# A planned four-layer graph kernel: bank preference in the planner, one opening of four block products, eps inside the squares, a later preamble step

## The chip, the core and the metric

The kernel runs on one core of one Trainium2 chip. A core has a matrix engine (TensorE, PE in the profile, with its weight loads shown apart as PEld), a vector engine (DVE), an activation engine (ACT), a general engine (POOL) and a queue for transfers (SP). Each engine works through its own instructions in a fixed order; semaphores make one engine wait for another. Matmul results land in PSUM, which is used here as eight banks of 128 x 512 fp32 values. The metric is the device time of one execution in microseconds, the median of several runs.

## The reference

The input is x, 64 graphs of 256 nodes with 128 features, and one 256 x 256 adjacency matrix A for all of them; everything is fp32. Four layers follow each other, and after each comes a layer norm of "x plus the layer":

```
layer 0: x W0 + sum over k=1..3 of (A^k x)(Wk + Wk+3)      x = LN(x + layer0)
layer 1: A (x W) + b                                        x = LN(x + layer1)
layer 2: D^-1/2 (A + I) D^-1/2 x W^T + b                    x = LN(x + layer2)
layer 3: h = x; five times:
           m = A h;  u = h U3^T + b
           z = sigmoid([m, m] W3^T + b + u);  r = sigmoid([m, m] W4^T + b + u)
           hv = tanh([m, m] W5^T + b + (r h) U5^T + b)
           h = (1 - z) h + z hv                             x = LN(x + h)
LN(v) = (v - mean) / sqrt(var + 1e-5) over the features
```

## The kernel before

**Tiling.** The 64 graphs are cut into 32 groups of two; a group is named by the number of its first graph (0, 2, 4 to 62). A group's activations fill one tile of 128 x 512: two graphs, two halves of the nodes, 128 features. Ten groups are in work at a time (`ACTIVE`), so that PE always finds a group that is ready. For later groups, transposed copies are made by a DVE transpose, a store to device memory and a load back (`tx`, `dx`, `xT` for the input; `th`, `dh`, `h` or `hT` in the steps of layer 3; `tn`, `dn`, `hn` at the end).

**The product with A.** `propagate` multiplies a tile by A. With both operands cut into 2 x 2 blocks, `seven` does this with seven block products in place of eight. POOL makes the sums of blocks of h (`ts01`, `ts2`, `ts3`, tiles `ts` and `tq`); the sums of A's blocks (`s_aT`, `s_a2T`, `s_anT`, `s_aTp`) are made once, on DVE, in the preamble (`block_sums`). The products share one bank, `ps` (in the profile `pmq`, `pm`, `pmg` for layer 0, layers 1 and 2, and layer 3). PE does them in four calls: `first` is one product and opens the bank, `middle` is the three that use POOL's sums, `more` is one that is added onto the first, `rest` is two. Between them ACT copies the first product (`us`), because `more` then changes it, DVE forms the sums `post11`, `post12`, `post13` and `post2` (L642, L645, L648, L652), and ACT copies a part of the bank into `m` (L664). `rest` writes where DVE and ACT read before, so it waits for them.

**Gates.** In a step of layer 3, `pr` gets two products, with m (`w4`) and with hT (`u3`); ACT makes r; DVE makes rh = r hT; `ph` gets products with m and with rh (the `u5` product); `pr` gets one more with m (`w34`), which turns it into the input of z. Then ACT makes z and hv, and DVE makes d = hv - hT, e = z d and the new hT (all L729).

**Norms.** The weights are centred in the preamble so that the outputs of the layers have mean zero. `normalise_centred` then needs only the mean square: four `Square` activations on ACT with scale C^-1/2 and an accumulated sum (L515; C is 128), EPS added on POOL (L519), the power -1/2 on POOL (L520), four scalings on ACT (L531). The last six groups end in `closing`, which gathers h and y by matmuls into a bank `s` and takes the same way, with the final product on DVE (L574). The other groups of the last layer use bn_stats on DVE (`statistics`, L491 to L502, L551).

**What sets the order.** Nothing is written out by hand: each piece of work is an `Op` with an engine, a cost in ns, a lag, a rank, a function that issues it, and the tiles that it reads and writes. `Plan.order` simulates the engines. It takes again and again, over all engines, the operation with the smallest key, and so fixes the order on each engine as well as the slot that each tile gets:

```
key = (max(at, t0), op.rank, op.seq)
```

`at` is when the inputs are ready and a slot of each needed kind is free, `t0` when the engine is free, and the rank of a group's operation is its number (for the last seven groups nearly equal, with a part that grows as the group moves on). Of the operations that could start at the same time the oldest group's goes first. Preamble operations (`pre`) have ranks of their own: -9 and -8 for A transposed and squared (aT, a2T), -7 for the first layer's weights (`w0s`), 0.3 for the normalised adjacency (`degree`, the power, `rows` L334, the PE transpose `p_an` L259, `columns` L338), 2.1 for the transposed weights of later layers (`transposed`, tiles `p_w2u3T` and `p_w435u5T`). The transposes into `p_w2u3T` use two loads, raw_w2 and raw_u3.

Of the kernel before, what the change touches and what calls it, by code (L numbers as in the profile page):

```python
# [8 lines left out]
F32 = mybir.dt.float32  # L9
AF = mybir.ActivationFunctionType  # L10
OP = mybir.AluOpType
AX = mybir.AxisListType

P = 128
# [9 lines left out]
EPS = 1e-5  # L24
# [26 lines left out]
class Plan:  # L51
# [32 lines left out]
    def order(self):  # L84
        free = {}
        pool = {k: [(0.0, i) for i in range(n)] for k, n in self.slots.items()}
        left = {op: len(op.deps) for op in self.ops}
        placed = {op: [v for v in op.vals if v.kind != "const"] for op in self.ops}
        after = {op: [] for op in self.ops}
        for op in self.ops:  # L90
            for d in op.deps:
                after[d].append(op)
        open_ = {}
        ready = {}
        for op in self.ops:
            if not left[op]:
                ready.setdefault(op.engine, []).append((0.0, op))
        done = []
        while any(ready.values()):
            best = None  # L100
            for e, waiting in ready.items():
                t0 = free.get(e, 0.0)
                pick = None
                for at, op in waiting:
                    need = {}
                    for v in placed[op]:
                        if v.slot is None:
                            need[v.kind] = need.get(v.kind, 0) + 1
                    short = False
                    for k, n in need.items():  # L110
                        if len(pool[k]) < n:
                            short = True
                            break
                        at = max(at, sorted(pool[k])[n - 1][0])
                    if short:
                        continue
                    key = (max(at, t0), op.rank, op.seq)
                    if pick is None or key < pick[0]:
                        pick = (key, op)
                if pick and (best is None or pick[0] < best[0]):  # L120
                    best = pick
            assert best, "the plan is stuck"
            (start, _, _), op = best
            ready[op.engine] = [w for w in ready[op.engine] if w[1] is not op]
            op.start, op.end = start, start + op.cost + op.lag
            free[op.engine] = start + op.cost
            for v in placed[op]:
                if v.slot is None:
                    pool[v.kind].sort()
                    v.slot = pool[v.kind].pop(0)[1]  # L130
                    open_[v] = len(v.users)
                open_[v] -= 1
                if not open_[v]:
                    pool[v.kind].append((max(u.end for u in v.users), v.slot))
            for n in after[op]:
                left[n] -= 1
                if not left[n]:
                    at = max(d.end for d in n.deps)
                    ready.setdefault(n.engine, []).append((at, n))
            done.append(op)  # L140
        assert len(done) == len(self.ops)
        return sorted(done, key=lambda op: (op.start, op.seq))


def pe_cost(columns, n=1):
    return n * 2 * (max(columns, P) / 1.2 + 2)
# [11 lines left out]
def kernel(  # L158
# [30 lines left out]
    nc = tc.nc  # L189
    B, N, C = x.shape  # L190
# [43 lines left out]
    half = const.tile([P, Q], F32, name="half")  # L234
    nc.vector.memset(half, -0.5)


    early = constant("early", [P, Q])
    pre(-9, "ACT", 1500, lambda: nc.scalar.activation(early.ap, half, AF.Sigmoid), [], [early])
# [44 lines left out]
    w0s = constant("w0s", [P, 4, C])  # L284
# [55 lines left out]

    pre(0.3, "DVE", 1500, degree, [a_nat], [ahat, deg])
    pre(0.3, "POOL", 700, lambda: nc.gpsimd.tensor_tensor(dinv.ap, deg.ap, half[:, :T], op=OP.pow), [deg], [dinv])
    pre(0.3, "DVE", 600, rows, [ahat, dinv], [ahat])
    pre(0.3, "PE", 4 * 110, lambda: turn(p_an, ahat), [ahat], [p_an])
    pre(0.3, "DVE", 900, columns, [p_an, dinv], [anT])


# [92 lines left out]
    class Group:  # L440
# [68 lines left out]
        def spread_of(self, tag, s):  # L509

            y, ve, rs = self.val("w", "y" + tag), self.val("ve", "ve" + tag), self.val("rs", "rs" + tag)

            def squares():
                for q in range(self.q):
                    nc.scalar.activation(nat(y)[:, q, :], nat(s)[:, q, :], AF.Square, scale=C ** -0.5,  # L515
                                         accum_out=ve.ap[:, q:q + 1])

            def scales():
                nc.gpsimd.tensor_scalar(ve.ap, ve.ap, EPS, None, op0=OP.add)  # L519
                nc.gpsimd.tensor_tensor(rs.ap, ve.ap, half[:, :self.q], op=OP.pow)  # L520

            self.act(squares, [s], [y, ve], 295 * self.q)
            self.add("POOL", 1330, 100, scales, [ve], [ve, rs])
            return y, rs

        def normalise_centred(self, tag, s):
# [66 lines left out]
        def seven(self, tag, h, aTs, ins, blocks):  # L593

            sums = sums_of[aTs]
            ps, m = self.val("bank", "pm" + tag), self.val("w", "m" + tag)
            ts, tq, u = self.val("th", "ts" + tag), self.val("q", "tq" + tag), self.val("th", "us" + tag)
            w = self.val("q", "ws" + tag)  # L600

            def row(v, k):
                return v.ap[:, k * P:(k + 1) * P]

            def o(v, q, blocks=blocks):
                if v.kind == "q":
                    return v.ap.rearrange("p (k i) -> p k i", k=4)
                if blocks:
                    return v.ap.rearrange("p (k q i) -> p q k i", k=4, i=32)[:, q]
                return v.ap.rearrange("p (q k i) -> p q k i", k=4, i=32)[:, q]  # L610


            def ts01():
                nc.gpsimd.tensor_tensor(ts.ap[:, :2 * P].rearrange("p (x c) -> p x c", x=2), ins(h)[:, 1], ins(h)[:, :, 0],  # L614
                                        op=OP.subtract)

            def ts2():
                nc.gpsimd.tensor_tensor(row(ts, 2), ins(h)[:, 1, 1], row(ts, 0), op=OP.subtract)

            def ts3():  # L620
                nc.gpsimd.tensor_tensor(tq.ap, row(ts, 2), ins(h)[:, 0, 1], op=OP.subtract)

            def block(q, w, a, start=False):
                mm(row(ps, q), w, a, start, True, shared=True)

            def first():
                block(0, ins(h)[:, 0, 0], aTs.ap[:, 0, :P], True)

            def middle():
                block(2, row(ts, 0), sums.ap[:, 0, :])  # L630
                block(1, row(ts, 1), sums.ap[:, 2, :])
                block(3, row(ts, 2), sums.ap[:, 1, :])

            def more():
                block(0, ins(h)[:, 0, 1], aTs.ap[:, 1, :P])

            def rest():
                block(2, ins(h)[:, 1, 1], sums.ap[:, 3, :])
                block(1, tq.ap, sums.ap[:, 4, :])

            def post11():
                nc.vector.tensor_tensor(row(u, 0), row(u, 1), row(ps, 3), op=OP.add)  # L642

            def post12():
                nc.vector.tensor_tensor(row(w, 0), row(u, 0), row(ps, 1), op=OP.add)  # L645

            def post13():
                nc.vector.tensor_tensor(o(m, 3), o(w, 0, False), o(ps, 2, False), op=OP.add)  # L648

            def post2():  # L650
                both = o(u, 0, False)[:, None].to_broadcast([P, 2, 4, 32])
                nc.vector.tensor_tensor(o(m, slice(1, 3)), o(ps, slice(1, 3), False), both, op=OP.add)  # L652

            started = self.pe(pe_cost(P, 1), first, [h, aTs], [ps])
            kept = self.act(lambda: nc.scalar.copy(row(u, 1), row(ps, 0)), [ps], [u], 165)
            self.add("POOL", 830, 100, ts01, [h], [ts])
            self.add("POOL", 610, 100, ts2, [h, ts], [ts])
            self.add("POOL", 590, 100, ts3, [h, ts], [tq])
            self.pe(pe_cost(P, 3), middle, [ts, sums], [ps], True, (started,))
            self.pe(pe_cost(P, 1), more, [h, aTs], [ps], True, (kept,))  # L660
            self.dve(post11, [ps, u], [u], 215)
            self.dve(post12, [ps, u], [w], 215)
            self.dve(post13, [ps, w], [m], 215)
            self.act(lambda: nc.scalar.copy(o(m, 0), o(ps, 0, False)), [ps], [m], 165, True)  # L664
            self.pe(pe_cost(P, 2), rest, [h, tq, sums], [ps], True)
            self.dve(post2, [ps, u], [m], 340, True)
            return m
# [245 lines left out]
```

## Time and profile before

Time before: 1354.72 us, the median of three runs (1353.41 to 1354.8). The profiled execution spans 1350.3 us from the first to the last instruction.

| engine | busy us | share of the span | instructions |
|---|---|---|---|
| PE (matmul) | 1336.5 | 99% | 6553 |
| PEld (weights) | 928.3 | 69% | 6553 |
| DVE | 940.9 | 70% | 2304 |
| ACT | 758.1 | 56% | 2421 |
| POOL | 680.7 | 50% | 1097 |

Matmuls overlap in the engine's pipeline, so a PE that is busy 99% of the time isn't by that at its peak: the distance from one matmul's start to the next tells more than its duration. A line of the timeline gives start and duration in us, engine and line of the kernel, the output tile, the inputs, the shapes and the count; in brackets stands how long the engine was idle before, and what ended it. A line of the groups gives the total busy time and the mean of one in ns, and after the next bar the idle time before. Transfers are 134.96 MB in all, and the queue engines are busy a third of the time.

### The profile page before, as it was taken

The page shows a single profiled execution, that of the slowest core. Times are in us where ns is not written, and L with a number is a line of the kernel's source. Part 1 is how long each engine was busy: PE and PEld are TensorE (multiplying, and loading weights), DVE is VectorE, ACT ScalarE, POOL GpSimd, SP SyncE. Part 2 cuts the span into 40 slices and gives each one's busy share as a digit, 9 for nine tenths or more (in the row PEclk, how much of TensorE's full clock was granted, in tenths as well). Part 3 has the DMA queues.
Part 4 walks back from the last instruction along what each step waited for, and adds up shares of the span by engine and source line. Part 5 has one row for each costly group of instructions (what it writes and reads, how often), then busy time and mean ns, then how long its engine had stood idle before and what let it go on. Part 6 is the DMA issues. An engine that isn't in the chain of part 4 may idle for free.

```text
span 1350.3 us, 22012 instructions
## 1 busy us (share of the span) xinstructions
PE 1336.5 (99%) x6553; PEld 928.3 (69%) x6553; DVE 940.9 (70%) x2304; ACT 758.1 (56%) x2421; POOL 680.7 (50%) x1097
## 2 busy tenths in 40 slices
PE   8999999999999999999999999999999999999997
PEld 7886666676776766677666666676776776565554
DVE  5466677767667667865676776676666677877776
ACT  4675536467654556556565554474655686444445
POOL 5785425266742566247266443383653686233323
PEclk9999999999999999999999999999999999999999
DMA  6322334242522333333233433341332223333323
GB/s 175 109 71 71 94 94 128 77 128 78 147 78 77 111 95 118 115 106 100 64 110 110 127 100 98 94 137 56 110 102 63 82 85 121 87 106 95 93 78 110
DMA packets 269495, 134.96 MB, mean 100 GB/s; under 512 B 175776, under 2 KB 241056, under 8 KB 269376
## 3 DMA queue, kind: packets, MB, share of 16 engines
q1 hardware_dynamic: 269120, 133.42, 34.1%
q8 instruction: 53, 0.87, 0.3%
q14 instruction: 66, 0.54, 0.1%
q0 software_dynamic: 256, 0.13, 0.1%
HBM read 67.31 MB, written 65.80 MB: 99 GB/s over the span
## 4 chain that ended last, share of the span: by engine, by line
PE 95%; DVE 1%; DMA 1%; ACT 1%; issue 0%; SPq 0%; POOLq 0%; ACTq 0%; POOL 0%; DVEq 0%
PE pr L199 31%; PE ph L199 20%; PE pmg L199 19%; PE py L199 15%; PE pm L199 7%; PE pmq L199 3%; DMA x<-in_x_dram 1%; DMA w_raw<-in_L_gnn_weight_dram 0%; PE s L199 0%; DMA dx<-tx 0%; ACT y L515 0%; ACT y L551 0%; DVE s L543 0%; SPq L748 0%; DVE tx L745 0%
## 5 line engine op out<-in xcount | busy, mean ns | idle before, releaser
L199 PE MATMUL pr<-mg,w435u5T 128*128 128x512 f32 x640 | 319.8, 593 | 0.0
L614 POOL TENSOR_TENSOR tsg<-h 128x256 f32<-128x256 f32 x128 | 97.2, 760 | 292.5 <-DMA h<-dh 197.5
L722 ACT ACTIVATE r<-pr,bsum 128x512 f32<-128x512 f32 x160 | 109.7, 685 | 151.5 <-PE pr L199 150.7
L722 ACT ACTIVATE pr<-pr,bsum 128x512 f32<-128x512 f32 x160 | 105.5, 660 | 112.4 <-PE pr L199 109.3
L729 DVE TENSOR_TENSOR rh<-r,hT 128x512 f32<-128x512 f32 x160 | 122.7, 767 | 61.6 <-ACT r L722 60.7
L199 PE MATMUL ph<-rh,w435u5T 128*128 128x512 f32 x320 | 163.6, 594 | 0.0
L199 PE MATMUL ph<-mg,w435u5T 128*128 128x512 f32 x320 | 163.3, 592 | 0.0
L199 PE MATMUL pr<-hT,w2u3T 128*128 128x512 f32 x320 | 163.0, 593 | 0.0
L729 DVE TENSOR_TENSOR d<-ph,hT 128x512 f32<-128x512 f32 x160 | 109.7, 686 | 76.1 <-ACT ph L722 73.0
L199 PEld LDWEIGHTS pr<-mg,w435u5T 128*128 128x128 f32 x640 | 109.4, 191 | 65.3 <-issue 53.3
L722 ACT ACTIVATE ph<-ph,bsum 128x512 f32<-128x512 f32 x160 | 105.6, 660 | 60.4 <-PE ph L199 59.9
L531 ACT ACTIVATE y<-s,rs 128x128 f32<-128x128 f32 x384 | 122.1, 392 | 11.0 <-POOL rs L520 10.7
L515 ACT ACTIVATE y<-s 128x128 f32<-128x128 f32 x396 | 116.7, 299 | 16.9 <-DVE s L538 14.9
L199 PEld LDWEIGHTS pmg<-s_aTp,tsg 128*128 128x128 f32 x768 | 101.8, 192 | 33.5 <-issue 28.5
L652 DVE TENSOR_TENSOR mg<-pmg,usg 128x256 f32<-128x256 f32 x160 | 67.0, 419 | 72.7 <-PE pmg L199 70.4
L199 PEld LDWEIGHTS pmg<-aTp,h 128*128 128x128 f32 x512 | 87.1, 197 | 39.4 <-issue 29.2
L729 DVE TENSOR_TENSOR pr<-pr,d 128x512 f32<-128x512 f32 x157 | 108.7, 692 | 1.5
L520 POOL TENSOR_TENSOR rs<-ve,half 128x4 f32<-128x4 f32 x99 | 104.1, 1052 | 8.3
L519 POOL TENSOR_SCALAR ve<-ve 128x4 f32<-128x4 f32 x99 | 23.2, 234 | 166.6 <-ACT y L515 166.3
L729 DVE TENSOR_TENSOR hT<-hT,pr 128x512 f32<-128x512 f32 x157 | 106.1, 676 | 1.3
L199 PE MATMUL pmg<-s_aTp,tsg 128*128 128x128 f32 x768 | 106.2, 275 | 0.0
L642 DVE TENSOR_TENSOR usg<-usg,pmg 128x128 f32<-128x128 f32 x160 | 45.2, 284 | 81.7 <-PE pmg L199 47.7
(181 smaller groups left out, 2816.9 us busy)
## 6 DMA issues: line engine op xcount, KB each, us to landing
dh<-th SPq DMA_DIRECT2D x160, 256.0 KB, 2.0
h<-dh SPq DMA_DIRECT2D x256, 128.0 KB, 2.5
x<-in_x_dram SPq DMA_DIRECT2D x32, 256.0 KB, 3.4
hT<-dh SPq DMA_DIRECT2D x128, 64.0 KB, 2.0
out_dram<-y SPq DMA_DIRECT2D x32, 256.0 KB, 2.3
dx<-tx SPq DMA_DIRECT2D x30, 256.0 KB, 2.6
xT<-dx SPq DMA_DIRECT2D x60, 128.0 KB, 2.6
dn<-tn SPq DMA_DIRECT2D x29, 256.0 KB, 2.1
```

Source lines behind the costliest of these rows:

```text
L199: nc.tensor.matmul(o, lhsT, rhs, start=start, stop=stop, skip_group_check=shared)
L515: nc.scalar.activation(nat(y)[:, q, :], nat(s)[:, q, :], AF.Square, scale=C ** -0.5, accum_out=ve.ap[:, q:q + 1])
L519: nc.gpsimd.tensor_scalar(ve.ap, ve.ap, EPS, None, op0=OP.add)
L520: nc.gpsimd.tensor_tensor(rs.ap, ve.ap, half[:, :self.q], op=OP.pow)
L531: nc.scalar.mul(nat(y)[:, q, :], nat(s)[:, q, :], rs.ap[:, q:q + 1])
L614: nc.gpsimd.tensor_tensor(ts.ap[:, :2 * P].rearrange("p (x c) -> p x c", x=2), ins(h)[:, 1], ins(h)[:, :, 0], op=OP.subtract)
L642: nc.vector.tensor_tensor(row(u, 0), row(u, 1), row(ps, 3), op=OP.add)
L652: nc.vector.tensor_tensor(o(m, slice(1, 3)), o(ps, slice(1, 3), False), both, op=OP.add)
L722: self.act(lambda: nc.scalar.activation(t.ap, ps.ap, func, bias=bias[1], scale=1.0), [ps, bias[0]], [t], act_cost(self.width) + 100)
L729: self.dve(lambda: nc.vector.tensor_tensor(out(t), way(a), way(b), op=op), [a, b], [t])
```

## The change

There are four edits, and they meet in the planner.

1. The planner's key gets a second place, `opens`: 0 if the operation touches a bank that has a slot already, else 1. Among operations that could start at the same time, one that works on an open bank goes ahead of one that doesn't, whatever the rank. It is meant to bring banks back sooner. It holds for every engine: on ACT and DVE it puts work on banks ahead of work between SBUF tiles.
2. `first` and `middle` become one call, `opening`, of four products. The bank is thus opened only when POOL's sums are there, and is held for a shorter time; the ACT copy of the first product comes after the four.
3. The eps of the centred norm moves into the squares, as a bias of sqrt(EPS/C) from a constant tile `root`. Since the values have mean zero, the accumulated sum of (v C^-1/2 + sqrt(EPS/C))^2 is the mean square plus EPS. The POOL addition goes away, and the planned cost of the POOL operation falls from 1330 to 1040 ns.
4. `rows` of the normalised adjacency gets rank 0.9 and reads `w0s` as well, so that it stands behind the first layer's weights on DVE; the transposes into `p_an` get rank 1.1. This is meant to keep them out of the way of the first groups.

```diff
@@ Plan.order
-                    need = {}
+                    need, opens = {}, 1
                     for v in placed[op]:
                         if v.slot is None:
                             need[v.kind] = need.get(v.kind, 0) + 1
+                        elif v.kind == "bank":
+                            opens = 0
...
-                    key = (max(at, t0), op.rank, op.seq)
+                    key = (max(at, t0), opens, op.rank, op.seq)
...
+    root = const.tile([P, 1], F32, name="root")
+    nc.vector.memset(root, (EPS / C) ** 0.5)
...
-    pre(0.3, "DVE", 600, rows, [ahat, dinv], [ahat])
-    pre(0.3, "PE", 4 * 110, lambda: turn(p_an, ahat), [ahat], [p_an])
+    pre(0.9, "DVE", 600, rows, [ahat, dinv, w0s], [ahat])
+    pre(1.1, "PE", 4 * 110, lambda: turn(p_an, ahat), [ahat], [p_an])
@@ Group.spread_of
                     nc.scalar.activation(nat(y)[:, q, :], nat(s)[:, q, :], AF.Square, scale=C ** -0.5,
-                                         accum_out=ve.ap[:, q:q + 1])
+                                         bias=root[:, 0:1], accum_out=ve.ap[:, q:q + 1])
...
-                nc.gpsimd.tensor_scalar(ve.ap, ve.ap, EPS, None, op0=OP.add)
                 nc.gpsimd.tensor_tensor(rs.ap, ve.ap, half[:, :self.q], op=OP.pow)
...
-            self.add("POOL", 1330, 100, scales, [ve], [ve, rs])
+            self.add("POOL", 1040, 100, scales, [ve], [rs])
@@ Group.seven
-            def first():
+            def opening():
                 block(0, ins(h)[:, 0, 0], aTs.ap[:, 0, :P], True)
-
-            def middle():
                 block(2, row(ts, 0), sums.ap[:, 0, :])
                 block(1, row(ts, 1), sums.ap[:, 2, :])
                 block(3, row(ts, 2), sums.ap[:, 1, :])
...
-            started = self.pe(pe_cost(P, 1), first, [h, aTs], [ps])
-            kept = self.act(lambda: nc.scalar.copy(row(u, 1), row(ps, 0)), [ps], [u], 165)
...
-            self.pe(pe_cost(P, 3), middle, [ts, sums], [ps], True, (started,))
+            self.pe(pe_cost(P, 4), opening, [h, ts, aTs, sums], [ps])
+            kept = self.act(lambda: nc.scalar.copy(row(u, 1), row(ps, 0)), [ps], [u], 165)
```

More of the change, by code (lines that the diff above doesn't have):

```diff
@@ L122, in order @@
             assert best, "the plan is stuck"
-            (start, _, _), op = best
+            (start, *_), op = best
             ready[op.engine] = [w for w in ready[op.engine] if w[1] is not op]
```

## The prediction

> **What bounds the kernel now.** First the busy shares, then the chain that ended last (its shares by engine, then by line):
>
> ```profile
> PE 1336.5 (99%) x6553; PEld 928.3 (69%) x6553; DVE 940.9 (70%) x2304; ACT 758.1 (56%) x2421; POOL 680.7 (50%) x1097
> PE 95%; DVE 1%; DMA 1%; ACT 1%; issue 0%; SPq 0%; POOLq 0%; ACTq 0%; POOL 0%; DVEq 0%
> ```
>
> TensorE (PE) is the path for nearly the whole span. Busy time of pipelined matmuls says little about lost time, so I read their starts: from one start to the next the trace has 109 ns for 128 columns, 216 for 256 and 430 for 512. Over the 6,553 recorded matmuls these sum to 1312.8 us, and the change leaves the count and shapes alone. The other 37.5 us of the 1350.3 us span are 1.4 before the first matmul, 8.6 lost in the first 50 us, 20.6 lost from there to the last matmul, and 6.9 after it. Of the 20.6, some 14.3 are the 2 to 3 ns that a matmul costs beyond its columns (quiet slices of 50 us all lose about 0.55); real waits in the middle are thus about 6.2 us. Only those 6.2 and the two ends can change.
>
> The start and its stalls, in order of time (start, duration, and in brackets the idle time before):
>
> ```profile
> 6.41 2.34 SPq L229 DMA_DIRECT2D raw_u<-in_L_gnn_u_w_dram  x2
> 8.23 0.60 PE L674 MATMUL ptx<-ident,x 128*128 128x128 f32 x4
> 10.03 0.81 PE L259 MATMUL p_an<-ident,ahat 128*128 128x128 f32 x4 [1.20 <-DVE ahat L334]
> 11.11 3.62 PE L199 MATMUL pmq<-a2T,x 128*128 128x256 f32 x16
> ...
> 29.36 0.49 PE L199 MATMUL pmq<-s_a2T,x 128*128 128x128 f32 x2 [1.27 <-ACT mq L664]
> ...
> 36.00 0.46 PE L199 MATMUL pm<-s_aT,y 128*128 128x128 f32 x2 [0.68 <-DVE m L648]
> ...
> 39.73 0.94 PE L199 MATMUL py<-wb,m 128*128 128x128 f32 x6 [0.62 <-DVE m L652]
> ```
>
> p_an stands in PE's queue ahead of work that was ready. The end of the program:
>
> ```profile
> 1341.33 0.69 DVE L729 TENSOR_TENSOR e<-pr,d 128x512 f32<-128x512 f32 x1
> 1342.35 1.05 PE L199 MATMUL s<-less,e 128*128 128x128 f32 x8
> ...
> 1344.73 0.23 POOL L519 TENSOR_SCALAR ve<-ve 128x4 f32<-128x4 f32 x1 [1.35 <-ACT y L515]
> 1345.04 1.04 POOL L520 TENSOR_TENSOR rs<-ve,half 128x4 f32<-128x4 f32 x1
> 1346.12 0.69 DVE L574 TENSOR_TENSOR y<-s,rs 128x512 f32<-128x512 f32 x1 [2.01 <-POOL rs L520]
> ```
>
> After the last matmul: squares on ACT, eps and power on POOL, product on DVE, store. Here the eps instruction is on the path. Last, the three kinds of ACTIVATE on 128x128:
>
> ```profile
> L531 ACT ACTIVATE y<-s,rs 128x128 f32<-128x128 f32 x384 | 122.1, 392 | 11.0 <-POOL rs L520 10.7
> L515 ACT ACTIVATE y<-s 128x128 f32<-128x128 f32 x396 | 116.7, 299 | 16.9 <-DVE s L538 14.9
> L551 ACT ACTIVATE y<-s,mv,rs 128x128 f32<-128x128 f32 x116 | 47.6, 484 | 0.2 <-POOL mv L502 0.2
> ```
>
> No operand from memory beside the data (L515): 299 ns; one (L531): 392; two (L551): 484.
>
> **What the Trainium skill says.** "ScalarE: Activation LUTs", section "What ACT_TABLE_LOAD costs": each `[128,1]` pointer operand adds about 93 ns to an ACTIVATE. The trace agrees: steps of 93 and 92 ns. "TensorE: Matmul & The Clock Gate", section "Wait — 56ns, not 53.3ns?": a pass of N columns takes N/2.4 GHz plus about 2.5 ns when warm. A recorded fp32 matmul of 512 columns at 430 ns fits two such passes (431 by its figures). "PSUM — Partial Sum Buffer", section Specifications: eight banks per partition; the planner hands out these eight, and the trace of before names no wait on a bank as such.
>
> **The change part by part.**
> *Adjacency later.* In the changed order p_an stands behind the first group's products (near 23 us), where its rows (DVE) are long done. But the w2/u3 transposes (23.4 us before) now come straight after the second ptx, ahead of pmq: the plan finds PE free there and takes their loads as landed. They wait for raw_u3. That load is issued at 6.41 and, by the tile's view, lands 4.8 us later, at 11.2. So PE: ptx twice (the second x lands at 2.28 + 6.9 = 9.2), done 9.65; w2 until 9.9; wait until 11.2; u3; pmq from about 11.45 instead of 11.11. One wait takes the other's place: +0.35, and with the differing work counted (0.33 of w2u3 in place of 0.44 of p_an) +0.45. Behind it the order runs without a wait up to `rest` of group 4's seven-product form (groups carry the number of their first graph: 0, 2, 4 to 62), whose write waits for DVE's L648. On DVE that now stands behind tx of group 12, which waits for its x; x can be issued only once dx of group 8 is out. With the trace's durations: tx of group 4 at 19.3 (1.5 earlier than before, since columns and the five sums of anT follow later), x of 8 lands 23.7, its tx ends 24.4, the xT issues keep the queue until 25.4, x of 12 lands about 29.2, tx ends 29.95, L648 ends 30.25. PE gets there at 28.95 and waits 1.35, as before (1.43). The later stalls of before (0.84+0.17 at 36.0, 0.79 at 39.7, 0.28 at 41.7, together 2.1) and some 0.3 of smaller ones don't recur by the same count, because PE has `opening` and `more` of groups 6, 8 and 10 in between. Sum at 45 us: +0.45 - 0.1 - 2.1 - 0.3 = about -2.0; bounds -3.0 (x lands half a microsecond sooner and u3 too) and +0.5 (each tx holds DVE as it did before).
>
> *Four products in one go, banks preferred.* Nothing is added or taken from PE. Its order gives the round trips more room: from the last product of a step to the next step's first three sums there were 12.9 us of PE work at the least, now 14.0; from the last block to the gate product (5th percentile) 0.87, now 1.08. Against it, from `opening` to `more` there are now only 0.65 to 0.9 us of other PE work in many cases; the ACT copy between (0.26) with two hand-overs needs about 0.5. I take -1.0 of the 6.2 us (0 to -3).
>
> *Eps as bias.* POOL loses 99 x 234 ns = 23 us, off the path since it is 50% busy. ACT gets a pointer operand 396 times: 396 x 93 = +37 us, +0.37 per squares. The planner's 295 ns per tile is unchanged, so it places work as if this cost nothing. In the trace of before, 77 of 90 squares are followed by the next ACT operation with under 0.37 us between, so that much is handed on: to a gate r 32 times, to copies of m some 48. How much reaches PE: the result that a matmul waits for is under 0.2 us early in 21 of 160 cases for the candidate product (L729 rh) and in 33 of 254 for the last blocks. About 0.02 us per delayed operation, 100 of them: +1.7; bounds 0 (all absorbed) and +5 (each r handed on in half the cases with 0.2). Middle together: +0.7, -3 to +5.
>
> *The end.* It was 6.9 us after the last matmul. In the changed order DVE's last part reads rh, y of 58, d and e of 60, the sum of 56, d of 62, bn_stats of 56, e of 62; before, both statistics came ahead of d and e of 62. ACT puts y of 54 (1.65) ahead of the last two hv. From the end of pr's u3 product of 62: r 0.2 + 0.69, y 1.65, hv 0.66, then six DVE operations of 0.69 to 0.86 (4.3), hand-overs 0.2: 7.7 us to e of 62; PE has 6.05 us of work there. So PE waits 1.55 before its last product (none before: e was 0.33 early). Then squares take 1.6 instead of 1.2 (+0.4), POOL saves 0.31, ACT's y of 56 and its store now run into the last store on the SP queue (+0.4). Sum +2.1; bounds 0.3 (DVE's turn comes as before) and +2.8.
>
> Forecast: 1354.7 - 2.0 + 0.7 + 2.1 = 1355.5 us: no change that can be measured.
>
> **The rivals.**
> A, faster: the looser order removes half of the middle's 6.2 us and ACT's gaps swallow the bias (-3.0), start -2.0, end +0.5: 1350.2. For it: ACT is idle 44%, POOL is freed, distances grew. Against: handed-on delay after 77 of 90 squares; at most 6.2 can be won there.
> B, slower: ACT becomes the wait that ends last in front of PE. Middle +4, start -1.0, end +2.4: 1360.1. For it: r starts as soon as PE has u3 out (137 of 160 within 0.1 us), so a busy ACT delays it at once, and the planner doesn't know of the longer squares. Against: DVE too is slower than planned (0.28 against 0.215 us for 128 columns), and that cost only part of 6.2 us.
> C: the start wins nothing, as raw_u3 and tx just take the old places (+0.45), the rest as forecast: 1358.0.
>
> **How the numbers follow.** Forecast 0.50, A 0.23, B 0.19, C 0.08. Faster means under 1352.0, slower over 1357.4. A lies almost wholly below 1352.0, B and C above 1357.4; the forecast's own spread gives each side 0.02: faster 0.25, same 0.46, slower 0.29. About half of A lies under 1350.6 and a little less than half of B over 1359.8; these ends leave out 2 in 10.
>
> **What would show it.** Right: L515's successor at about 392 ns and L519 gone; PE idle near 10 to 11.2 us on raw_u3 and again near 29 to 30; the wait of p_an gone; little else until 45 us; in the last 10 us a wait of PE on DVE's e of over 1 us, and out stores close together. Wrong: waits of PE on ACT (r, m, us) that add up to more than 4 us in the middle, or slices there all at 0.55. The forecast fails most easily in the middle, where it rests on early and late results of the old order.

## The result and the profile after

The changed kernel takes 1359.29 us (median of 4, 1358.16 to 1359.96) against 1354.76 for the kernel before, run beside it: ratio 1.0035, 95% interval 1.0018 to 1.0052. That is 4.5 us slower. It lies half a microsecond inside the upper end of the forecast range, 1359.8; the likeliest case, no measurable change, did not come.

The page of the changed kernel, busy times and the chain that ended last:

```profile
PE 1339.3 (99%) x6553; PEld 929.1 (68%) x6553; DVE 945.5 (70%) x2305; ACT 791.3 (58%) x2421; POOL 652.4 (48%) x998
PE 92%; ACT 3%; DVE 1%; issue 1%; DMA 1%; POOL 0%; SPq 0%; POOLq 0%; DVEq 0%; ACTq 0%
```

PE has the same 6553 matmuls. ACT is up by 33 us, POOL down by 28, and ACT's share of the chain went from 1% to 3%. The groups of ACT:

```profile
L520 ACT ACTIVATE y<-s,root 128x128 f32<-128x128 f32 x396 | 153.6, 394 | 14.0 <-DVE s L542 11.8
L535 ACT ACTIVATE y<-s,rs 128x128 f32<-128x128 f32 x384 | 122.7, 397 | 6.3 <-POOL rs L524 5.9
```

A square takes 394 ns instead of 299, 95 ns more where the forecast had 93. The start, in order of time:

```profile
7.47 0.60 PE L675 MATMUL ptx<-ident,x 128*128 128x128 f32 x4
11.18 0.77 PE L675 MATMUL ptx<-ident,x 128*128 128x128 f32 x4 [3.11 <-DMA x<-in_x_dram]
11.75 0.76 PE L201 MATMUL p_w2u3T<-less,raw_w 128*128 128x128 f32 x2
13.40 0.47 PE L404 MATMUL p_w2u3T<-ident,raw_u 128*128 128x128 f32 x1 [0.89 <-DMA raw_u<-in_L_gnn_u_w_dram]
13.67 5.97 PE L201 MATMUL pmq<-a2T,x 128*128 128x256 f32 x16
...
34.30 0.46 PE L201 MATMUL pmq<-s_a2T,x 128*128 128x128 f32 x2 [0.53 <-ACT y L520]
```

The wait of p_an is gone. PE waits 3.11 us for the second x and 0.89 for raw_u3 instead, and then the 16 matmuls of pmq take 5.97 us where they took 3.62: for most of them the starts are 427 ns apart instead of 216. The end:

```profile
1347.07 1.16 PE L201 MATMUL s<-less,e 128*128 128x128 f32 x8 [0.21 <-DVE e L730]
...
1349.31 0.40 ACT L520 ACTIVATE y<-s,root 128x128 f32<-128x128 f32 x1
1349.45 1.01 POOL L506 TENSOR_TENSOR rs<-ve,half 128x4 f32<-128x4 f32 x1
...
1350.69 1.01 POOL L524 TENSOR_TENSOR rs<-ve,half 128x4 f32<-128x4 f32 x1
1351.73 0.69 DVE L578 TENSOR_TENSOR y<-s,rs 128x512 f32<-128x512 f32 x1 [1.52 <-POOL rs L524]
1352.45 0.37 SPq L847 DMA_DIRECT2D out_dram<-y  x1
1352.91 0.46 SPq L844 DMA_DIRECT2D out_dram<-y  x1
```

The last squares end at 1349.8, but the power of 62 starts only at 1350.69, because the power of 56 (L506) came in front of it on POOL. The last store is issued behind that of 56.

I measure PE's loss as in the prediction: distances between matmul starts, less the distances of a full pipeline. For 512 columns the trace of before has 429 ns more often than 430, and the forecast's sum of 1312.8 us fits 429; with the 430 that it writes, the sum is 1314.5 and every middle below about 1.7 us smaller. Differences between kernels don't depend on it. Every run below is read with this table ("profiled" is the time of the execution that the losses are from; "start" is the first 50 us, "1050" the stretch from 1050 to 1150 us, "middle" all from 50 us to the last matmul, "tail" what follows it). Ratios are to the kernel before, run in between on the same chip.

```
kernel                          median   ratio [95%]             profiled start middle 1050 tail
before                          1354.76                          1352.22    8.6   20.6  3.1  6.9
before, second profile                                           1353.12    9.4   20.6  3.1  6.9
changed                         1359.29  1.0035 [1.0018,1.0052]  1358.81   10.6   23.3  5.2  8.6
changed, eps a plain number     1354.00  0.9993 [0.9985,1.0001]  1353.87   10.9   18.6  2.9  8.2
changed, eps added on POOL      1351.90  0.9977 [0.9969,0.9985]  1352.10   10.5   16.8  2.6  8.6
changed, planner told           1358.38  1.0026 [1.0018,1.0034]  1357.63   10.4   23.5  7.9  7.6
changed, adjacency early        1362.47  1.0055 [1.0042,1.0067]  1362.47   11.7   26.1  9.3  8.6
before + operand                1361.08  1.0040 [1.0026,1.0054]  1362.62   13.3   26.2  3.9  7.1
before + adjacency late         1354.17  0.9993 [0.9985,1.0001]  1354.61   12.0   19.5  1.9  6.8
before + bank preference        1356.63  1.0016 [1.0009,1.0024]  1354.87   10.4   21.6  4.9  6.7
before + four products          1351.25  0.9979 [0.9970,0.9988]  1354.11   13.6   17.5  3.4  6.9
plain number, no preference     1356.97  1.0019 [1.0013,1.0026]  1357.70   10.7   24.5  8.4  6.4
plain number, w2/u3 late        1352.67  0.9985 [0.9978,0.9992]  1351.47   11.4   16.1  2.1  7.9
plain, no preference, w2/u3 late 1355.86 1.0002 [0.9994,1.0010]  1355.86   12.3   21.0  6.8  6.5
```

### The profile page after: what moved, and what is told of

It reads as the page before. It is cut to its first block, busy times and chain, and to the rows that moved or that the text cites. A ratio compares the mean times of both kernels' runs of the same rounds, so it can differ in the third digit from the quotient of the medians.

```text
span 1356.8 us, 21702 instructions
## 1 busy us (share of the span) xinstructions
PE 1339.3 (99%) x6553; PEld 929.1 (68%) x6553; DVE 945.5 (70%) x2305; ACT 791.3 (58%) x2421; POOL 652.4 (48%) x998
## 4 chain that ended last, share of the span: by engine, by line
PE 92%; ACT 3%; DVE 1%; issue 1%; DMA 1%; POOL 0%; SPq 0%; POOLq 0%; DVEq 0%; ACTq 0%
PE pr L201 30%; PE ph L201 20%; PE pmg L201 18%; PE py L201 15%; PE pm L201 6%; PE pmq L201 3%; ACT y L520 2%; ACT y L535 0%; DMA raw_u<-in_L_gnn_u_w_dram 0%; SPq L231 0%; POOL rs L524 0%; DVE s L542 0%; DMA h<-dh 0%; DMA dh<-th 0%; POOL rs L506 0%
## 5 line engine op out<-in xcount | busy, mean ns | idle before, releaser
L520 ACT ACTIVATE y<-s,root 128x128 f32<-128x128 f32 x396 | 153.6, 394 | 14.0 <-DVE s L542 11.8
L201 PEld LDWEIGHTS pmg<-aTp,h 128*128 128x128 f32 x512 | 90.8, 196 | 68.0 <-issue 39.2
L644 DVE TENSOR_TENSOR usg<-usg,pmg 128x128 f32<-128x128 f32 x160 | 45.5, 286 | 83.3 <-PE pmg L201 59.6
L201 PE MATMUL pmg<-aTp,h 128*128 128x128 f32 x512 | 99.4, 280 | 1.2 <-ACT usg L660 1.1
L796 POOL TENSOR_TENSOR yb<-y,wb 128x512 f32<-128x512 f32 x64 | 83.6, 1306 | 30.4 <-ACT y L535 29.4
L201 PEld LDWEIGHTS ph<-rh,w435u5T 128*128 128x128 f32 x320 | 57.8, 190 | 57.9 <-issue 42.5
```

Of the source, the lines that this page charges most:

```text
L201: nc.tensor.matmul(o, lhsT, rhs, start=start, stop=stop, skip_group_check=shared)
L796: nc.gpsimd.tensor_tensor(nat(yb), nat(y), bias[1][:, None, :].to_broadcast([P, self.q, C]), op=OP.add)
```

## The experiments

**The operand, in the new order.**

```diff
-   bias=root[:, 0:1], accum_out=ve.ap[:, q:q + 1])
+   bias=(EPS / C) ** 0.5, accum_out=ve.ap[:, q:q + 1])
```

> The changed kernel with eps as a plain number in the instruction (bias=(EPS/C)**0.5) in place of the [128,1] operand; every engine's order is that of the changed kernel. Squares should fall from 394 to about 299 ns. Theory 'the operand delays ACT, and PE waits for it': PE's loss from 50 us to the last matmul falls from 22.8 to about 20.5 us and the end loses 0.4, so about 1356.6 us. Rival 'the new order itself makes the waits, ACT's gaps swallow the operand': middle stays within 0.5 us of 22.8, about 1359.0 us.

Measured: 1354.00 us, middle 18.6, tail 8.2. Its squares take 299 ns:

```profile
L520 ACT ACTIVATE y<-s 128x128 f32<-128x128 f32 x396 | 116.8, 299 | 16.6 <-DVE s L542 14.0 <-PE s L201 2.2
```

All that separates it from the changed kernel is the operand, and that is 5.3 us by the medians: 4.7 in the middle, 0.4 in the tail by the profiles. The theory stands, at twice the size that it gave the middle (2.3), and its rival fell. Since both kernels have the same matmuls in the same order, the losses can be subtracted matmul by matmul: 6.0 us of new waits, most of them 0.1 to 0.5 us, and 1.4 us of waits that went (1.0 of that at two places that come up again below, at 99 and 234 us). About half of the new ones stand in front of `pmg<-aTp,h` and `pmg<-aT,y`, the form that `more` has. What PE waited for, the changed kernel first (columns: waiting, its releaser, us in total, times, longest):

```profile
PE pmg L201 <- ACT usg L660: 1.4, 4, 0.6
...
PE pm L201 <- ACT us L660: 0.4, 1, 0.4
```

And with the plain number:

```profile
PE pmg L201 <- ACT usg L660: 0.6, 2, 0.5
PE pm L201 <- DVE m L650: 0.5, 2, 0.3
```

One such place in the changed kernel, ACT and PE:

```profile
657.72 0.41 ACT L520 ACTIVATE y<-s,root 128x128 f32<-128x128 f32 x1
...
658.89 0.39 ACT L520 ACTIVATE y<-s,root 128x128 f32<-128x128 f32 x1
...
659.27 0.24 ACT L660 COPY usg<-pmg 128x128 f32<-128x128 f32 x1
659.57 0.50 PE L201 MATMUL pmg<-aTp,h 128*128 128x128 f32 x2 [0.23 <-ACT usg L660]
```

And the same work with the plain number:

```profile
656.76 0.31 ACT L520 ACTIVATE y<-s 128x128 f32<-128x128 f32 x1
...
657.65 0.30 ACT L520 ACTIVATE y<-s 128x128 f32<-128x128 f32 x1
...
657.94 0.24 ACT L660 COPY usg<-pmg 128x128 f32<-128x128 f32 x1
658.24 0.50 PE L201 MATMUL pmg<-aTp,h 128*128 128x128 f32 x2
```

From the first square to the copy: 1.55 us with the operand, 1.18 without. The 0.37 us of four squares reach PE in full, since the copy stands between `opening` and `more` and PE has little else to do there. Near 435 us three sets of squares stand in a row with one copy between, and the delay on ACT adds up to 1.0 us, of which the first matmul behind them loses 0.47.

**The operand, in the old order.** `root` and the bias as in the change, POOL's addition gone, the planner's costs and operands as before, so that no order changes:

```diff
+   bias=root[:, 0:1], accum_out=ve.ap[:, q:q + 1])
...
-   nc.gpsimd.tensor_scalar(ve.ap, ve.ap, EPS, None, op0=OP.add)
```

> The kernel before with eps as the pointer bias and POOL's addition gone, but the planned costs and operands kept, so that every engine's order is that of before. Only the +95 ns of 396 squares and the -0.23 us of 99 POOL operations act. Theory 'the operand reaches PE in any order': +1.7 to +2.5 us in the middle, +0.05 at the end (0.4 more for squares, 0.3 less on POOL): about 1356.7. Rival 'it hurts only where the new order leaves no room': within 0.5 us of before, about 1354.8.

Measured: 1361.08, 6 us slower than before; the middle went from 20.6 to 26.2, and the rival, no cost in the old order, fell. By matmul, the new waits stand here before `ph<-rh` and `pr<-mg` (1.3 and 1.4 us more) and before the last blocks of layer 3 (1.1 more). But this run changes two things at once, the operand and the POOL addition that goes, so the 5.6 us are the price of edit 3 in the old order and not of the operand alone. (In the new order the middle differs by 6.5 with and without edit 3, see the next run.) Not all of these waits are ACT's: before `ph<-rh` PE waits for DVE's rh, which takes longer here because POOL is at work beside it. Before, two rh in a row near 454 us, and the same two in this run:

```profile
453.31 1.62 DVE L729 TENSOR_TENSOR rh<-r,hT 128x512 f32<-128x512 f32 x2
...
460.30 2.53 DVE L731 TENSOR_TENSOR rh<-r,hT 128x512 f32<-128x512 f32 x2
462.29 1.12 PE L199 MATMUL ph<-rh,w435u5T 128*128 128x512 f32 x2 [0.18 <-DVE rh L731]
```

How much of the 5.6 us is the operand's is open: a plain number in the old order was not run.

**Eps back on POOL.** The changed kernel with edit 3 undone where it runs; each engine's order stays but for the addition:

```diff
-   bias=root[:, 0:1], accum_out=ve.ap[:, q:q + 1])
+   accum_out=ve.ap[:, q:q + 1])
...
+   nc.gpsimd.tensor_scalar(ve.ap, ve.ap, EPS, None, op0=OP.add)
    nc.gpsimd.tensor_tensor(rs.ap, ve.ap, half[:, :self.q], op=OP.pow)
```

> The changed kernel with eps added on POOL again, ahead of the power (no operand in the squares), every engine's order otherwise that of the changed kernel. So each chain squares, rs, product is 0.23 to 0.31 us longer than with the plain number (1354.0), at no load on ACT. Theory 'the operand hurts by ACT's occupancy, which holds up the copies and gates queued behind the squares': only the tail's 0.3 and little more, 1354.5. Rival 'it hurts by the longer chain to y': 0.3 of the operand's 0.37 us gives about 4 us, 1358.

Measured: 1351.90, ratio 0.9977. The rival fell: a longer chain to y costs 0.4 us in the tail and nothing in the middle. My theory named the engine rightly but missed the size: with one more POOL instruction in each of 99 chains the kernel is some 2 us faster than with the plain number. So the order of the changed kernel (edits 1, 2 and 4, with the smaller planned cost of edit 3) wins 3 us over before, and what edit 3 does on the engines turns that into a loss of 4.5.

Where the 2 us are: matmul by matmul, 1.16 of the 1.8 us that the middles differ by come from two places, at 99 and at 234 us. In both, DVE's rh runs beside POOL. With the plain number, DVE, POOL and the PE that waits in the end:

```profile
232.09 1.83 DVE L730 TENSOR_TENSOR rh<-r,hT 128x512 f32<-128x512 f32 x1 [1.58 <-ACT r L723]
232.11 1.26 POOL L796 TENSOR_TENSOR yb<-y,wb 128x512 f32<-128x512 f32 x1
234.65 0.62 PE L201 MATMUL pmg<-aTp,h 128*128 128x128 f32 x3 [0.46 <-ACT usg L660]
```

And with the addition on POOL, at the same work:

```profile
231.26 1.03 DVE L728 TENSOR_TENSOR rh<-r,hT 128x512 f32<-128x512 f32 x1 [1.85 <-ACT r L721]
231.70 1.72 POOL L794 TENSOR_TENSOR yb<-y,wb 128x512 f32<-128x512 f32 x1
233.19 0.51 PE L201 MATMUL pmg<-aTp,h 128*128 128x128 f32 x3
```

rh takes 0.69 us when POOL does nothing. In the first trace it takes 1.83 and POOL's yb an undisturbed 1.26; in the second rh takes 1.03 and yb, at 1.72, most of the loss. Behind rh on DVE stands L644, behind that ACT's copies mg and usg, and then PE. The Trainium skill, "GPSIMD Engine Reference", section "1. Specifications", says that GpSimd's SBUF interfaces are shared with VectorE, with contention for DVE instructions that have two SBUF inputs; rh has two. The traces agree, and show that one waits for the other to end: each rh that takes over 0.76 us (36 with the plain number, 38 with the addition) ends 0.55 us after the end of a POOL instruction that ran beside it. So a few tenths of a microsecond on POOL decide whether rh comes ahead of yb or behind it. For these two places that is shown; for the rest of the 2 us it is not. Nor is the addition better for DVE as such: all 160 rh together take 122.9 us with the plain number and 122.2 with the addition. What differs is which of the meetings stand in front of PE.

**The planner told.**

```diff
-   self.act(squares, [s], [y, ve], 295 * self.q)
+   self.act(squares, [s], [y, ve], 390 * self.q)
```

> The changed kernel, operand kept, with the planned cost of the squares raised from 295 to 390 ns a tile, so that the planner places work for the ACT time that the operand takes. Theory 'half of the operand's 5.3 us comes from a plan that doesn't know of it': about 1356.7. Rival 'ACT's added 37 us can't be hidden by another order': 1359, within what another order gives by chance (1 to 2 us).

Measured: 1358.38, within the interval of the changed kernel. The rival stands for the total. The stretches say more: from 50 to 1050 us the loss is 13.2, as with the plain number (13.3; the changed kernel has 15.6), while from 1050 to 1150 us it is 7.9 against 5.2. That looks like a plan that hides the operand where ten groups are in work and loses it again where the last groups run together. It isn't shown: four orders without the operand (the plain number above and the three runs with it below) lose between 11.6 and 14.1 us from 50 to 1050 us, so another order alone moves this stretch as much.

**The adjacency, each way.** Edit 4 undone in the changed kernel, and edit 4 alone in the kernel before:

```diff
-   pre(0.9, "DVE", 600, rows, [ahat, dinv, w0s], [ahat])
-   pre(1.1, "PE", 4 * 110, lambda: turn(p_an, ahat), [ahat], [p_an])
+   pre(0.3, "DVE", 600, rows, [ahat, dinv], [ahat])
+   pre(0.3, "PE", 4 * 110, lambda: turn(p_an, ahat), [ahat], [p_an])
```

> The changed kernel with the normalised adjacency put back to its old place (ranks 0.3, no wait for w0s); the first 20 us of PE's order are those of before, the tail is that of the changed kernel. Theory 'the start pays for the wait for x and raw_u3 plus a cold PE clock': PE's 4 first pmq take 3.6 us again instead of 6.0, the loss in the first 50 us falls from 10.6 to about 8.6, 1357.3 us in all. Rival 'the cold clock is made up for by stalls that the changed order loses later in the start': no change against the changed kernel within 0.5 us, 1359.0.

> The kernel before with only the adjacency moved later. Its PE order in the first 20 us is that of the changed kernel. Theory 'the wait for x and raw_u3 and the cold clock cost 2': loss in the first 50 us about 10.6, in all 1356.8. Rival 'neutral at the start': 1354.8; and if the move gives what it was made for, 1353.5.

Measured: 1362.47 without it, 3.2 us slower than the changed kernel by the medians (2.7 by the ratios, whose intervals overlap), and 1354.17 with it alone, 0.7 faster than before (the interval reaches no change). The theory that edit 4 costs 2 us at the start fell: without it, p_an waits 3.3 us and the clock drops as well (start 11.7). Most of the 3.2 is not at the start at all: the stretch from 1050 to 1150 us loses 9.3 instead of 5.2.

**Before once more.**

> The kernel before once more, for a second profile of its start. In the first one w0_raw landed at 8.4 us and the loss in the first 50 us was 8.6; every other profile so far shows w0_raw at 10.2 to 10.8. Theory 'the early landing was chance': w0_raw lands after 10 us here too, p_an waits 3 to 4 us instead of 1.2, and the first 50 us lose 11 to 13. Rival 'the changed programs make the loads land later': 8.4 and 8.6 again.

Measured, one execution at 1353.12. The lines that answer to the start of before:

```profile
9.89 0.38 DVE L287 TENSOR_TENSOR w0s<-w_raw,ident 128x128 f32<-128x128 f32 x1 [4.64 <-DMA w_raw<-in_L_gnn_weight_dram]
11.47 0.70 PE L259 MATMUL p_an<-ident,ahat 128*128 128x128 f32 x3 [2.50 <-DVE ahat L334]
```

w0_raw's first use is at 9.9 us instead of 8.4, p_an waits 2.5 us instead of 1.2, and the start loses 9.4. That is between the two expectations; it shows that the start of before varies, and that the first profile caught a quick one. In neither of the two does the clock drop in the start. Middle and tail agree to 0.1 us in the two profiles.

**The w2/u3 transposes later**, with the plain number:

```diff
-   pre(2.1, "PE", len(parts_) * 110, run, [*parts_, less], [ps])
+   pre(2.1, "PE", len(parts_) * 110, run, [*parts_, less, *((anT,) if raw["w2"] in parts_ else ())], [ps])
```

> The changed kernel with eps as a plain number, and the w2/u3 transposes held back until the normalised adjacency is done, so that they no longer stand ahead of pmq and wait for raw_u3. Theory 'the wait for raw_u3 (1.3 us) is on the path of the start': loss in the first 50 us 9.6 instead of 10.9, 1352.7 in all against 1354.0. Rival 'PE makes up for it at the later wait for the squares of group 0 (0.7 to 1.5 us)': 1354.0.

Measured: 1352.67. The total is as the theory said, the reason is not. Its start:

```profile
11.36 0.65 PE L672 MATMUL ptx<-ident,x 128*128 128x128 f32 x4 [3.11 <-DMA x<-in_x_dram]
11.85 3.62 PE L201 MATMUL pmq<-a2T,x 128*128 128x256 f32 x16
...
33.60 0.77 PE L201 MATMUL pmq<-s_a2T,x 128*128 128x128 f32 x2 [3.52 <-DVE mq L647]
```

And the busy times of a stretch that begins in that last wait (the 0.51 is the granted clock):

```profile
33.20:36.60 3.40, 3.00 (x14) 3.04 (x15) 1.39 (x4) 1.45 (x11) 2.33 (x5) 0.51 0.76 205
```

The wait for raw_u3 is gone, and so is the slow clock under pmq. PE then stands 3.52 us at `rest` of group 4, behind DVE's L647, and the clock falls there instead, to half for some 3.4 us; the start loses 11.4, no less than with the transposes early (10.9). The gain is in the middle, 16.1 instead of 18.6, where the plan came out differently.

**The two order edits alone**, each in the kernel before:

```diff
...
-   key = (max(at, t0), op.rank, op.seq)
+   key = (max(at, t0), opens, op.rank, op.seq)
```

> The kernel before with only the planner's preference for operations whose bank is already taken. Tail and start are nearly those of before. Theory 'the looser order wins up to 2 us in the middle, half of it from each of the two order edits': middle loss about 19.5 instead of 20.5, 1354.0. Rival 'only both together win': 1354.9; 'it costs': above 1356.

```diff
-   started = self.pe(pe_cost(P, 1), first, [h, aTs], [ps])
...
-   self.pe(pe_cost(P, 3), middle, [ts, sums], [ps], True, (started,))
+   self.pe(pe_cost(P, 4), opening, [h, ts, aTs, sums], [ps])
```

> The kernel before with only the four products of the seven-product form in one go (the ACT copy after them). Theory 'the looser order wins up to 2 us, half of it here': about 1354.0. Rival 'the short distance from the four products to the next one makes new waits on the ACT copy us': waits of pmg and pm on us of 2 us and more, 1356.5.

Measured: the preference alone costs 2 us (1.0016; 4.9 instead of 3.1 in the stretch from 1050), as the second rival had it; the four products alone win 3 us (0.9979; the middle falls from 20.6 to 17.5), three times what the theory gave them. (The profiled execution of that run, at 1354.11, is 2.9 us slower than its median, with 13.6 lost in the start.) The waits on us that the rival there feared are a single one of 0.6 us.

**Without the preference**, in the changed kernel with the plain number, and then with the transposes late too:

> The changed kernel with eps as a plain number and without the planner's preference for banks already taken; four products in one go and the later adjacency stay. Its DVE tail has both statistics of 56 ahead of e of 62 again, as before. Theory 'the bank preference costs in this company as it did alone (+2)': tail 6.9 instead of 8.2, middle 17.5 to 18.5 instead of 18.6, about 1351.5. Rival 'alone it costs, but with the four products it pays': 1354.0 or more.

> As g3, and the w2/u3 transposes held back until the adjacency is done. Theory 'holding them back wins about 1.3 as it did with the bank preference': g3 less 1.3, about 1350.2. Rival 'the win there was chance of the planned order, the start only hands the wait on to the wait near 34 us': same as g3.

Measured: 1356.97 and 1355.86. With the preference they were 1354.00 and 1352.67. So the rival stands: the preference that costs 2 us alone wins 3 us beside the other edits, although its DVE order at the end costs 1.4 to 1.8 us of tail (8.2 and 7.9 instead of 6.4 and 6.5). Without it the loss sits in the stretch from 1050 to 1150 us (8.4 and 6.8). In the first of the two the clock is at half there from 1091.6 to 1095.1 us, which by my estimate is 1.7 of the 8.4. Two of its lines:

```profile
1090.13 0.49 PE L199 MATMUL pm<-aT,y 128*128 128x128 f32 x2 [1.00 <-ACT us L655]
...
1118.46 0.94 PE L199 MATMUL py<-w2u3T,m 128*128 128x128 f32 x6 [1.60 <-DVE m L649]
```

Late transposes won 1.3 and 1.1 us in the two orders by the medians, which fits the theory's number, though the intervals of the first pair overlap; the profile of the first pair puts it in the middle, and in the second pair the start rose by 1.6 too, so I don't call it a gain of the start.

**What beats both kernels.** The changed kernel with eps left on POOL (1351.90, 0.9977) and the kernel before with the four products alone (1351.25, 0.9979) are each 3 us faster than before; their intervals don't part them. Eps on POOL together with late transposes was not tried.

## Why the prediction was wrong in its likeliest case

*The step that failed: "About 0.02 us per delayed operation, 100 of them: +1.7".* The operand's price (93 ns, 396 times, +37 us of ACT) was right. What reaches PE was mis-sized: 4.7 us in the middle instead of 1.7, close to the upper bound of +5. Two things were left out. I counted how early rh and the last blocks come, not the us copies, which the new order in many cases puts between two PE calls 0.65 to 0.9 us apart; I wrote down that distance under the order edits and didn't carry it to the operand. And I took each delay as a single one of 0.37, where sets of squares follow each other and add up to 1.0. Rival B named the mechanism, gave 1360.1, and was the nearest, in part by luck: its middle (+4, measured +2.7) and its start (-1.0, estimated below at about 0) are off in opposite directions.

*"POOL loses 23 us, off the path".* In this order taking the addition away cost about 2 us, 1.8 of it in the middle. More than half of that, 1.16 us, comes from when POOL meets DVE at two places; the cause of the rest stays open. A busy share of 50% said nothing on that.

*The start, -2.0.* As far as it can be estimated, it came out near zero. The profiles say +2.0 (8.6 to 10.6), but the profiled execution of before was 2.5 us quicker than the median. Its middle and tail repeat in a second profile, so I put all of this into the start and estimate its usual loss there at 8.6 + 2.5 = 11.1; for the changed kernel, which has one profile only, the same step gives 10.6 + (1359.29 - 1358.81) = 11.1 as well. The other profiles point the same way: in the six with the adjacency early the start loses 8.6 to 13.6 us, 11.2 in the mean, and in the six with it late and the w2/u3 transposes ahead of pmq 10.4 to 12.0, 10.9 in the mean. The steps "the second x lands at 9.2" and raw_u3 "at 11.2" failed: 11.1 and about 13.3. Both were read from one execution, with its quick loads. The clock was not in the sum at all: it cost 2.3 us in pmq. It fell in the first 20 us in all six profiles of the second kind, and in three of the six with the adjacency early. What held is the other half of the argument: PE has to wait for the group-4 `rest`, and what is won ahead of it is waited for there (0.5 us in the changed kernel, behind ACT's squares and not the L648 of the prediction; 3.5 with the transposes late; at 34.3 and 33.6 us). Rival C's "the start wins nothing" is what happened there.

*The order, -1.0.* Right in sign. With edit 3 undone on the engines the middle loses 16.8 instead of 20.6, -3.7 with edit 4's share in it, beyond the bound of -3. That the two edits can't be priced one by one, +2 and -3 alone and -3 together with edit 4, was in no step.

*The end, +2.1.* Measured +2.2: 1.7 in the tail and 0.5 of the wait for e. That it fits is luck, since the parts were others. PE stood idle for e 0.2 us instead of 1.55 (by the starts of the two matmuls behind the wait it lost 0.37 and 0.10): e of 62 was done 7.1 us after the u3 product instead of 7.7, and PE had some 7.0 us of work there, where I had counted 6.05. The power of 62 stood 0.9 us behind that of 56 on POOL, which I hadn't seen, and the two stores together cost 0.9 instead of 0.4 (from the end of the last product to the end of the span 4.4 us, 3.5 before); the squares (+0.3, said 0.4) and the POOL addition (-0.3) were about as said.

*Together.* Against the forecast the operand came out 3.0 us dearer, the POOL addition 1.8 and the start, by the estimate, 2.0, and the order 2.7 us better. So the likeliest case failed as much in the start as in the middle, and there the better order hid a good part of edit 3's price.

The signs in "what would show it" were met as follows: p_an's wait gone, squares at 394, stores close together. Not met: PE's wait for raw_u3 came at 12.5 to 13.4 us instead of 10 to 11.2, that for the `rest` at 34 instead of 29 to 30, and there was no wait for e of over 1 us. And "waits of PE on ACT that add up to more than 4 us", named as what would prove me wrong, come near that only in the difference of two runs, where 6.0 us are new and 4.7 net, not all of them on ACT directly: the waits view names just 1.8 us of ACT's copies in the middle of the changed kernel, since much of the rest comes in pieces of about 0.1 us, many of them the longer distance between the first two matmuls behind a wait, which that view doesn't count.

## What to carry to other kernels

An operand that adds 95 ns to an instruction costs what stands behind it in its engine's queue: look for short copies between two calls of the bounding engine, and for runs of the lengthened instruction, before counting how idle the engine is. A constant belongs in the instruction as a number where it can be; here that left the square at 299 ns. When a planner sets the order, price an edit only by a run of the whole, repeat the profile of the start before reading landing times from it, and compare kernels of the same order matmul by matmul.

## What the runs showed of the hardware

- A square with a number as bias takes 299 ns, as with none; with a tile as bias 394. The Trainium skill, "ScalarE: Activation LUTs", section "What ACT_TABLE_LOAD costs", gives 93 ns for each pointer operand; 95 here, with an accumulated sum beside it.
- The granted clock fell to half for stretches of some 3.4 or 6.9 us in the first 50 us of eleven of the fourteen profiles, in the changed kernel from 11.6 to 18.4 us; matmuls of 256 columns then start 427 ns apart, some eleven of them there, and the mean granted clock of the first 50 us is 0.93. The Trainium skill, "TensorE: Matmul & The Clock Gate", section "What's actually happening", puts the fall to half the clock after an idle window of about 3.4 us. The stretches have about that length or twice it, but that figure alone doesn't tell when the clock falls here: 3.11 us alone left the 16 matmuls of pmq at 3.62 us (transposes late), while 2.75 us alone, in the same kernel without the preference, were followed by a fall:

```profile
10.90 0.66 PE L670 MATMUL ptx<-ident,x 128*128 128x128 f32 x4 [2.75 <-DMA x<-in_x_dram]
11.40 5.31 PE L199 MATMUL pmq<-a2T,x 128*128 128x256 f32 x16
```

- DVE's rh with two SBUF inputs takes 0.69 us alone and up to 1.83 beside POOL in these two traces. An rh that takes over 0.76 us ends 0.55 us after a POOL instruction ended; the one that waits can also be POOL (yb 1.72 instead of 1.26).
- The landing of the first loads varies by 1.5 us between two executions of the same program (w0_raw used at 8.4 and 9.9 us).
